# A slot planner that counts the piece it lets in, and VectorE pieces moved behind the slot's product

## The chip, the cores and the metric

The kernel runs on one NeuronCore of a Trainium2 chip, as one launch. The time is that of the device for the whole program, in microseconds (us). The engines are called by their short names: PE (TensorE), DVE (VectorE), ACT (ScalarE), POOL (GpSimd) and SP (SyncE, which here issues DMAs). Each engine has its own list of instructions and works it off in order; semaphores tie the lists together.

## The reference

Four images of 384 channels and 48 x 48 pixels in fp32 go through four layers. Each layer first normalises by groups of channels and adds its result to its input:

```python
x = x + mamba(_gn(x))        # L0: projections, a causal conv of 4 taps, a scan with 16 states, LayerNorm
x = x + fft_ffn(_gn(x))      # L1: 1x1 conv, 8x8 rfft2 * filter, irfft2, 3x3 depthwise, gelu gate, 1x1 conv
x = x + dwconv11(_gn(x))     # L2: depthwise 11x11 whose taps come from 4 moving points
x = x + moe(_gn(x))          # L3: 4 experts, two 1x1 convs each, top-2 routing over all pixels
```

The core of L0 runs over 2304 time steps for each of 768 channels and 16 states:

```python
dA = exp(dt * A); h = dA * h + dt * B * x; y = sum_over_states(h * C)
```

## The kernel before

**L0 in slots.** `scans` (from line 556) cuts each image into 5 chunks of 460 or 464 time steps, and each chunk into 96 slots. A slot is one state of one tile of 128 channels. There are 4 x 5 x 96 = 1920 slots. The order in which a slot's instructions stand is written out by hand in a loop (lines 1074 to 1113) under a manual schedule. In slot `u`: DVE runs the recurrence as one scan instruction (`scan`, L850); the product with C is made by DVE in the same slot (`product_now`, L870) in somewhat over half of the slots, and by POOL a slot later (`product`, L879) in the others, which are called slow; ACT copies the last column as carry (`keep`, L864) and makes the decay of a later slot by an exponential (`decay`, L826); POOL makes the driving term of slot `u + 3` (`drive`, L837); PE transposes and adds the product of slot `u - 3` or `u - 5` into a PSUM bank (`turned`, L770). The carry of a slot with a DVE product is copied after that product. The decay lies in PSUM; there are three such banks at most, and six buffers for g.

**Everything else is fed into the slots.** While image b + 1 is in L0, the later layers of image b fill the gaps: `later` (L1, L2 and the scores of L3) and `experts` (L3's experts 0 to 3). Their work is written as generators, called tasks. A task yields ahead of each step what the step is: `("act",)`, `("dve",)`, `("pool",)` or `("pe", weight, ring)`. The weight is an estimate of its time on PE in us. L0's own side work (projections, gates, output projection, LayerNorm) is written in the same way.

**Who lets a step in.** There are three lanes: `aux` (L0's own, not bound by the meter), `one` (`later`) and `two` (`experts`). `Lane.step` goes over its tasks and emits the next step of each that may go. One `Meter` (L62 to L69) keeps PE's backlog: every slot takes 2.3 off, adds 0.44 for the slot's own transposes, and each step let in adds its weight. A bound lane's PE step is let in while the backlog is not over 2.0; how large the step itself is isn't asked. A PE step also needs a free PSUM bank (`Ring`: three banks for pieces and one for accumulators; a bank is free again once its reader has been emitted). `Task.move` sets the slot from which the next step may go.

**Order within a slot** (lines 1080 to 1113): the lanes' ACT steps; collect; the scan; the transposes of earlier slots; the lanes' other steps, DVE's among them; the DVE product with its carry; decay; POOL's product; drive; DMA issues for B and C. So a lane's DVE step stands between the slot's scan and the slot's product.

**After the last slot**, lane `two` still holds expert blocks of image 2, and all later layers of image 3 remain. They are fed by the same lanes without scans (loop at lines 1816 to 1824), until the routing over all pixels (`route_all`) and the experts of image 3 (`all_experts`, L1709 and L1726) close the program. This stretch is called the tail below. A block of an expert is two products, `ph` and `pout`, of 9 matmuls each (L1609), every one of them two records in the profile.

The DVE steps that the change touches, each of which reads a PSUM tile that PE has written: `gate` (L907), the filter of L1 (L1225), the residual of L1 (L1311, L1313), that of L2 (L1437, L1439), an expert's bias (L1587) and an expert's sum (L1641 for experts 1 to 3, L1644 for expert 0).

Of the kernel before, what the change touches and what calls it, by code (L numbers as in the profile page):

```python
# [68 lines left out]
        self.value = max(0.0, self.value - self.each) + given  # L69


class Task:

# [3 lines left out]
        self.steps, self.next, self.ended, self.after = None, None, False, 0  # L79

    def move(self, slot=0):

        self.after = slot + 1 if self.next and self.next[0] == "act" else 0
        try:
            if self.steps is None:
                self.steps = self.make()
            self.next = (*next(self.steps), 0, None, None)[:4]
        except StopIteration:
            self.ended = True


class Lane:
# [4 lines left out]
        self.meter = meter  # L97
        self.bound = bound

    def step(self, act, slot, at=0):  # L100
        for task in self.active:
            if task.ended:
                continue
            kind, weight, ring, when = task.next
            if (kind == "act") != act or task.after > slot:
                continue
            if weight and self.bound and self.meter.value > self.meter.limit:
                continue
            if (ring and not ring[0].free(ring[1])) or (when and not when()):
                continue  # L110
            self.meter.value += weight
            task.move(slot)
        self.active = [t for t in self.active if not t.ended]
        while (
            self.queue and len(self.active) < self.width and self.queue[0].at <= max(at, slot)
            and all(t.ended for t in self.queue[0].needs)
        ):
            task = self.queue.pop(0)
            task.move()
            if not task.ended:  # L120
                self.active.append(task)

    def drain(self, slot, others=()):
        n = 0
        while self.queue or self.active:
            self.meter.value = 0.0
            for act in (True, False):
                for lane in (self, *others):
                    lane.step(act, slot + n, 1 << 30)
            n += 1  # L130
            assert n < 20000, "stuck"

# [7 lines left out]
def tile_layers(ctx: ExitStack, tc: tile.TileContext, a: dict, out: bass.AP):  # L140
# [272 lines left out]
    with ExitStack() as first:  # L413
# [142 lines left out]
        def scans(wk, mm, ring, meter, place, lanes, begin):  # L556
# [338 lines left out]
            def gate(i, m):  # L895
                (b, t), c = G[i], st[i]
                n = CHUNKS[t]
                w = n // TT
                yield ("pe", 0.45, (ring, 1))
                ps, r = ring.take(f"pyb{b}_{t}_{m}")  # L900
                for k in range(TT):
                    nc.tensor.transpose(
                        ps[:, bass.ts(k, w)], c["yt", m][:w, bass.ts(k, P)], ident[:w, :w]
                    )
                yield ("dve",)
                zm = c["zs"][:, m, :n]
                nc.vector.tensor_tensor(zm, ps[:, :n], zm, ALU.mult)  # L907
                ring.done(r)
# [134 lines left out]
            def ready(u):  # L1043

                i, p, m, s, _ = where(u)
                task, n = named.get(("steps", i, p)), 0
                while task and not task.ended:
                    for act in (True, False):
                        for lane in (aux, *lanes):
                            lane.step(act, u + n, 1 << 30 if lane is aux else 0)  # L1050
                    n += 1
                    assert n < 1000, "stuck"

# [9 lines left out]
            with tc.manual_schedule():  # L1063
                ordered[0] = True
                for k in range(3):
                    spread(k, 0)
                    spread(k, 1)
                for u in range(3):
                    drive(u)
                spread(3, 0)  # L1070
                for u in range(3):
                    decay(u)
                decays = 3
                for u in range(N + 6):
                    if u % LEN == 0 and u <= N:
                        plan(u // LEN, u)
                    if u < N and u % (LEN * NC) == 42 and u > 42:
                        begin(G[u // LEN][0])
                    place[0] = u
                    for lane in (aux, *lanes):  # L1080
                        lane.step(True, u)
                    for h, e in ((1, u - 4), (0, u - 5)):
                        if 0 < e < N and e % PAIR == PAIR - 1:
                            collect(e, h)
                    if u < N:
                        scan(u)


                    meter.slot(0.44)
                    early = u % PAIR >= 8  # L1090
                    if early:
                        add(u - 5, True)
                        add(u - 3, False)
                    for lane in (aux, *lanes):
                        lane.step(False, u)
                    if u < N:
                        product_now(u)
                    if decays < N and decays <= u + (3 if decays < LEN * NC else 2):
                        decay(decays)
                        decays += 1  # L1100
                    if 0 < u <= N:
                        product(u - 1)
                    if u + 3 < N:
                        ready(u + 3)
                        drive(u + 3)
                    if not early:
                        add(u - 5, True)
                        add(u - 3, False)
                    if u % 2:
                        spread((u + 7) // 2, 0)  # L1110
                        spread((u + 5) // 2, 1)

                at = u
                while aux.queue or aux.active:
                    at += 1
                    meter.slot(0.0)
                    for act in (True, False):
                        for lane in (aux, *lanes):
                            lane.step(act, at)
                lanes[0].drain(at, lanes[1:])  # L1120
                place[0] = at
                ordered[0] = False
# [4 lines left out]
        def later(b, ring, accr):  # L1127
# [71 lines left out]
            def patches(hb, wb):  # L1199
# [21 lines left out]
                us, uk = ufs.take(f"uf{u_}")  # L1221
                nc.tensor.matmul(ps[:, :C], lhsT=dft_f, rhs=ts_, start=True, stop=True)  # L1222
                tps.done(tk)
                yield ("dve",)
                nc.vector.tensor_tensor(us, ps[:, :C], filt_t, ALU.mult)  # L1225
                ring.done(r)
                yield ("pe", 0.65, (ring, 1))
# [24 lines left out]
            def finish_strip(hb):  # L1252
# [46 lines left out]
                for ct in range(CT):  # L1299
                    yield ("pe", 1.3, (ring, 1))  # L1300
                    ps, r = ring.take(f"pb{b}_{hb}_{ct}")
                    nc.tensor.matmul(  # L1302
                        ps[:, :LB], lhsT=w[:, 0, bass.ts(ct, P)], rhs=act[:, 0, :],
                        start=True, stop=False,
                    )
                    nc.tensor.matmul(  # L1306
                        ps[:, :LB], lhsT=w[64:P, 1, bass.ts(ct, P)], rhs=act[64:P, 1, :],
                        start=False, stop=True,
                    )
                    yield ("dve",)  # L1310
                    nc.vector.tensor_add(x[:, ct, :], ps[:, :LB], x[:, ct, :])  # L1311
                    ring.done(r)
                    nc.vector.bn_stats(stats2[b % 2][:, ct, hb, :], x[:, ct, :])  # L1313
# [92 lines left out]
            def windows(ct, k, r, first, last, final):  # L1406
# [24 lines left out]
                    for h in range(2):  # L1431
                        lines.done(d["row", ct, r, h][1])
                if last:
                    yield ("dve",)
                    n = BANDS[k] * W
                    x, xk = d["xb", ct, k]
                    nc.vector.tensor_add(x[:, :n], d["acc2"][0][:, :n], x[:, :n])  # L1437
                    accr.done(d["acc2"][1])
                    nc.vector.bn_stats(stats3[b % 2][:, ct, k, :], x[:, :n])  # L1439
                    yield ("pool",)  # L1440
                    nc.sync.dma_start(x3d[b][of_band(ct, k)], x[:, :n])
                    xbs.done(xk)
# [104 lines left out]
        def experts(b, ring, rings):  # L1547
# [15 lines left out]
            def begin(e):  # L1563
# [12 lines left out]
                for m in range(CT):  # L1576
                    for k in range(CT):
# [4 lines left out]
                            start=k == 0,  # L1582
                            stop=k == CT - 1,
                        )
                yield ("dve",)
                nb = d["nb", e] = small.tile([P, CT], F32, name=f"nb1_{b}_{e}", tag="nb1")
                nc.vector.tensor_tensor(nb, b1_all[:, e, :], ps[:, :CT], ALU.subtract)  # L1587
                ring.done(r)
# [13 lines left out]
            def block(s, e):  # L1602
# [30 lines left out]
                done(("h", s, e))  # L1633
                if s == NS - 1:
                    done(("w", e))
                yield ("dve",)
                key = ("y" if e else "x", s, e)
                x = d[key][0]
                if e:
# [134 lines left out]
            )  # L1774

        ring, accr = psum("mm", 3), psum("acc", 1)
        meter = Meter(2.3, 2.0)
        one, two = Lane(8, meter), Lane(4, meter)

        def begin(b):  # L1780
# [12 lines left out]
        with (  # L1793
# [6 lines left out]
            at = place[0]  # L1800
            while not all(ring.read):
                at += 1
                for act in (True, False):
                    two.step(act, at)
            two.queue = held

        rt = first.enter_context(tc.tile_pool(name="route", bufs=1))
        with (
# [7 lines left out]
            while one.queue or one.active or two.queue or two.active:  # L1816
                at += 1
                meter.slot(0.0)
                if not (one.queue or one.active):
                    meter.value = 0.0  # L1820
                for act in (True, False):
                    for lane in (one, two):
                        lane.step(act, at)
            coef, whole = route_all(rt, mm)
            all_experts(
                NB - 1, wk,
# [117 lines left out]
```

## Time and profile before

| | us |
|---|---|
| median of 3 runs | 5437.34 |
| lowest, highest | 5428.49, 5438.78 |
| profiled execution, its own time | 5425.31 |
| its span | 5423.4 |
| first scan starts | 86.9 |
| last scan ends | 4525.0 |
| PE busy over the span | 4666.9 (86%) |
| DVE busy | 4053.8 (75%) |
| POOL busy | 3365.2 (62%) |
| ACT busy | 2985.2 (55%) |

The profile is that of one execution. Its page gives busy time by engine, the span in 40 slices, and groups of instructions with their mean time; the trace behind it can be asked for any stretch. A wait is put down to the instruction that ended it. A stretch of 96 slots, one chunk of L0, is the natural unit here: its bounds are the starts of every 96th L850. Chunks are numbered 0 to 19. Chunks 0 to 4 are image 0 and have L0's own work alone; from chunk 5 on the lanes have work of the later layers as well.

### The profile page before, as it was taken

Reading aid. Unit: us, or ns where it says so; the run is one execution under the profiler, and the core shown is the slowest. Engines: PE = TensorE matmul, PEld = TensorE weight load, DVE = VectorE, ACT = ScalarE, POOL = GpSimd, SP = SyncE. Lnnn points to the kernel's source line nnn. Section 1 sums busy time; section 2 is a strip of 40 time slices with the busy share of each in tenths; the row PEclk is TensorE's granted clock in tenths of the full one; section 3 lists DMA queues with packets and bytes.
Section 4 is the critical chain, followed back from the end, with each engine's and each line's share of the span. In section 5 each row is a group of like instructions: output and inputs, shape, how many; then the busy total and the mean of one; then the engine's idle time right before and its main releaser. Section 6 shows DMA issues by size and latency. Waiting matters only on the chain. (4 is left out here: it accounts for less than half of the span.)

```text
span 5423.4 us, 81753 instructions
## 1 busy us (share of the span) xinstructions
PE 4666.9 (86%) x27796; PEld 3676.0 (68%) x27796; DVE 4053.8 (75%) x5581; ACT 2985.2 (55%) x6632; POOL 3365.2 (62%) x3020
## 2 busy tenths in 40 slices
PE   5677677687678988988789999988899999999899
PEld 4444454454347767665678887765678878889799
DVE  5999989889998788899887778899977674452200
ACT  3565565565558765655467655665566653334321
POOL 3878878876678788765667678775777673000000
PEclk8788788788789999999899999999999999999899
DMA  4445445454345555644566566554655554543200
GB/s 123 138 136 148 127 128 146 126 150 132 106 129 150 146 161 164 177 143 139 155 169 176 149 170 171 156 158 129 170 157 169 157 167 143 166 140 112 64 27 23
DMA packets 628391, 758.95 MB, mean 140 GB/s; under 512 B 58869, under 2 KB 622181, under 8 KB 627582
## 3 DMA queue, kind: packets, MB, share of 16 engines
q1 hardware_dynamic: 617668, 751.98, 48.2%
q8 instruction: 221, 3.62, 0.3%
q10 hardware_dynamic: 10298, 1.67, 0.2%
q14 instruction: 204, 1.67, 0.1%
HBM read 663.81 MB, written 89.65 MB: 139 GB/s over the span
## 5 line engine op out<-in xcount | busy, mean ns | idle before, releaser
L837 POOL TENSOR_TENSOR bu<-u,B 128x460 f32<-128x460 f32 (+1 forms) x1920 | 2227.5, 1170 | 778.2 <-DVE g L850 395.5
L826 ACT ACTIVATE da<-dt,a_neg 128x460 f32<-128x460 f32 (+1 forms) x1920 | 1242.8, 649 | 281.9 <-DVE g L870 185.4
L770 PE MATMUL y<-ident,g 128*115 128x128 f32 (+1 forms) x7680 | 1140.2, 297 | 274.1 <-DVE g L870 164.1
L770 PEld LDWEIGHTS y<-ident,g 128*115 128x115 f32 (+1 forms) x7680 | 1011.0, 187 | 502.3 <-DVE g L870 199.2
L879 POOL TENSOR_TENSOR g<-g,C 128x460 f32<-128x460 f32 (+1 forms) x885 | 1030.5, 1164 | 276.8 <-ACT carry L864 270.4
L850 DVE TENSOR_TENSOR_SCAN da<-da,carry,bu 128x460 f32<-128x460 f32 (+1 forms) x828 | 971.3, 1173 | 133.3 <-ACT da L826 94.7
L850 DVE TENSOR_TENSOR_SCAN g<-da,carry,bu 128x460 f32<-128x460 f32 (+1 forms) x708 | 819.7, 1167 | 83.5 <-ACT da L826 35.3
L870 DVE TENSOR_TENSOR g<-da,C 128x460 f32<-128x460 f32 (+1 forms) x1035 | 653.9, 632 | 91.7 <-PE y L770 31.5
L864 ACT COPY carry<-da 128x1 f32<-128x1 f32 x828 | 130.5, 158 | 824.3 <-DVE g L870 821.2
L1609 PE MATMUL pout<-hr,we 128*128 128x144 f32 x3456 | 483.6, 296 | 41.7 <-ACT hr L1625 31.7
L1609 PEld LDWEIGHTS pout<-hr,we 128*128 128x128 f32 x3456 | 455.4, 196 | 64.9 <-ACT hr L1625 42.6
L1609 PE MATMUL ph<-xe,we 128*128 128x144 f32 x3456 | 470.1, 291 | 13.4 <-DMA xe<-x3d 7.5
L1609 PEld LDWEIGHTS ph<-xe,we 128*128 128x128 f32 x3456 | 446.8, 194 | 30.6 <-issue 7.6
L1416 PE MATMUL pc<-band,row 128*128 128x162 f32 (+14 forms) x3456 | 458.8, 287 | 6.3 <-ACT row L1403 6.0
L1416 PEld LDWEIGHTS pc<-band,row 128*128 128x128 f32 x3456 | 446.2, 196 | 11.9 <-ACT row L1403 7.5
L1274 DVE SCALAR_TENSOR_TENSOR dw<-pad,w_dw,dw 128x384 f32<-128x384 f32 x576 | 347.6, 614 | 17.6 <-ACT pad L1249 6.7
L642 PE MATMUL pin<-xch,w_inx 128*128 128x463 f32 (+2 forms) x720 | 327.9, 595 | 34.7 <-DMA xch<-in_x 15.2
L921 PE MATMUL po<-w_out,zs 128*115 128x384 f32 (+1 forms) x960 | 341.5, 499 | 6.9 <-DVE dt L750 6.4
L1625 ACT ACTIVATE hr<-ph,nb 128x144 f32<-128x144 f32 x576 | 176.4, 377 | 305.2 <-PE ph L1609 303.6
L674 PE MATMUL pinz<-xch,w_inz 128*128 128x460 f32 (+1 forms) x720 | 316.8, 578 | 0.0
L1383 ACT ACTIVATE rep<-x,br,wr 128x192 f32<-128x192 f32 x576 | 274.3, 541 | 4.2 <-issue 4.2
L661 DVE SCALAR_TENSOR_TENSOR xc<-pin,conv_w,xc 128x460 f32<-128x460 f32 (+1 forms) x360 | 249.2, 692 | 30.9 <-ACT xc L655 19.2
(202 smaller groups left out, 5797.6 us busy)
## 6 DMA issues: line engine op xcount, KB each, us to landing
B<-bcd SPq DMA_DIRECT2D x768, 230.0 KB, 3.5
C<-bcd SPq DMA_DIRECT2D x768, 230.0 KB, 3.7
B<-bcd SPq DMA_DIRECT2D x192, 232.0 KB, 3.7
C<-bcd SPq DMA_DIRECT2D x192, 232.0 KB, 4.2
xe<-x3d SPq DMA_DIRECT2D x192, 216.0 KB, 2.8
ye<-y3d SPq DMA_DIRECT2D x144, 216.0 KB, 2.8
y3d<-ye SPq DMA_DIRECT2D x96, 216.0 KB, 2.2
xs<-x1d SPq DMA_DIRECT2D x24, 576.0 KB, 4.6
```

The costliest lines, as they stand in the source:

```text
L642: nc.tensor.matmul(ps[:, lo : halo + n], lhsT=w_inx[:, k, bass.ts(j, P)], rhs=c["x"][:, k, lo : halo + n], start=k == 0, stop=k == CT - 1,)
L674: nc.tensor.matmul(ps[:, :n], lhsT=w_inz[:, k, bass.ts(j, P)], rhs=c["x"][:, k, DCONV - 1 : DCONV - 1 + n], start=k == 0, stop=k == CT - 1,)
L770: nc.tensor.matmul(c["y", m][:w, bass.ts(k, P)], lhsT=src[:, bass.ts(k, w)], rhs=ident, is_transpose=True, start=c["terms", m] == 1 and k ...
L826: nc.scalar.activation(da[:, :n], c["dt", p][:, m % 2, :n], AF.Exp, scale=a_neg[:, m, s : s + 1])
L837: nc.gpsimd.tensor_mul(bu[:, :n], c["u", p][:, m % 2, :n], live["B", u // 2][:, :n])
L850: nc.vector.tensor_tensor_scan(here[:, :n], da[:, :n], bu[:, :n], last if t else nil[:, 0:1], ALU.mult, ALU.add,)
L870: nc.vector.tensor_mul(live["g", u][:, :n], live["h", u][:, :n], live["C", u // 2][:, :n])
L879: nc.gpsimd.tensor_mul(g[:, :n], g[:, :n], live["C", u // 2][:, :n])
L921: nc.tensor.matmul(ps[:w, :C], lhsT=c["zs"][:, m, bass.ts(k, w)], rhs=w_out0[:, m, :], start=m == 0, stop=m == MT - 1,)
L1274: nc.vector.scalar_tensor_tensor(v, src, w_dw[:, ct, k : k + 1], v, ALU.mult, ALU.add)
L1416: nc.tensor.matmul(d["acc2"][0][:, : BANDS[k] * W].rearrange("p (h w) -> p h w", w=W)[:, lo - edges[k] : hi - edges[k], xlo:xhi], lhsT=d[" ...
L1609: nc.tensor.matmul(ps[:, bass.ts(m, EB)], lhsT=w[:, k, bass.ts(m, P)], rhs=of[:, k, :], start=k == 0, stop=k == CT - 1,)
```

## The change

Three things are changed.

1. `Lane.step` compares the backlog with the piece's weight added, `value + weight > limit`, and the limit goes from 2.0 to 3.7.
2. A third phase is added to each slot. DVE steps that read what PE has made for them yield `("late",)`, and the lanes' late steps are emitted after `product_now`. DVE's other steps stay ahead of the product.
3. `Task.move` holds every kind of step, and not ACT's alone, to one a slot, so that a PE step and its late reader do not fall into one slot.

```diff
+PHASE = {"act": 0, "late": 2}
...
     def move(self, slot=0):
-
-        self.after = slot + 1 if self.next and self.next[0] == "act" else 0
+        self.after = slot + 1 if self.next else 0
...
-    def step(self, act, slot, at=0):
+    def step(self, phase, slot, at=0):
         for task in self.active:
             if task.ended:
                 continue
             kind, weight, ring, when = task.next
-            if (kind == "act") != act or task.after > slot:
+            if PHASE.get(kind, 1) != phase or task.after > slot:
                 continue
-            if weight and self.bound and self.meter.value > self.meter.limit:
+            if weight and self.bound and self.meter.value + weight > self.meter.limit:
                 continue
...
                     for lane in (aux, *lanes):
-                        lane.step(True, u)
+                        lane.step(0, u)
...
                     for lane in (aux, *lanes):
-                        lane.step(False, u)
+                        lane.step(1, u)
                     if u < N:
                         product_now(u)
+                    for lane in (aux, *lanes):
+                        lane.step(2, u)
...
-        meter = Meter(2.3, 2.0)
+        meter = Meter(2.3, 3.7)
```

In `gate`, `patches`, `finish_strip`, `windows`, `experts.begin` and `block`, the step ahead of the lines named above changes in the same way:

```diff
-                yield ("dve",)
+                yield ("late",)
```

All other loops over phases (`drain`, `ready`, the loops of the tail) go over three phases in place of two.

More of the change, by code (lines that the diff above doesn't have):

```diff
@@ L126, in drain @@
             self.meter.value = 0.0
-            for act in (True, False):
+            for phase in range(3):
                 for lane in (self, *others):
-                    lane.step(act, slot + n, 1 << 30)
+                    lane.step(phase, slot + n, 1 << 30)
             n += 1
@@ L1047, in ready @@
                 while task and not task.ended:
-                    for act in (True, False):
+                    for phase in range(3):
                         for lane in (aux, *lanes):
-                            lane.step(act, u + n, 1 << 30 if lane is aux else 0)
+                            lane.step(phase, u + n, 1 << 30 if lane is aux else 0)
                     n += 1
@@ L1116, in scans @@
                     meter.slot(0.0)
-                    for act in (True, False):
+                    for phase in range(3):
                         for lane in (aux, *lanes):
-                            lane.step(act, at)
+                            lane.step(phase, at)
                 lanes[0].drain(at, lanes[1:])
@@ L1223, in patches @@
                 tps.done(tk)
-                yield ("dve",)
+                yield ("late",)
                 nc.vector.tensor_tensor(us, ps[:, :C], filt_t, ALU.mult)
@@ L1309, in finish_strip @@
                     )
-                    yield ("dve",)
+                    yield ("late",)
                     nc.vector.tensor_add(x[:, ct, :], ps[:, :LB], x[:, ct, :])
@@ L1433, in windows @@
                 if last:
-                    yield ("dve",)
+                    yield ("late",)
                     n = BANDS[k] * W
@@ L1584, in begin @@
                         )
-                yield ("dve",)
+                yield ("late",)
                 nb = d["nb", e] = small.tile([P, CT], F32, name=f"nb1_{b}_{e}", tag="nb1")
@@ L1635, in block @@
                     done(("w", e))
-                yield ("dve",)
+                yield ("late",)
                 key = ("y" if e else "x", s, e)
@@ L1802, in tile_layers @@
                 at += 1
-                for act in (True, False):
-                    two.step(act, at)
+                for phase in range(3):
+                    two.step(phase, at)
             two.queue = held
@@ L1820, in tile_layers @@
                     meter.value = 0.0
-                for act in (True, False):
+                for phase in range(3):
                     for lane in (one, two):
-                        lane.step(act, at)
+                        lane.step(phase, at)
             coef, whole = route_all(rt, mm)
```

## Prediction

> **What bounds the kernel now.** I read the page's busy times and slices first, then the busy times by stretch of 96 slots, then the waits of DVE and ACT, then one place in order of time. From the page:
>
> ```profile
> PE 4666.9 (86%) x27796; PEld 3676.0 (68%) x27796; DVE 4053.8 (75%) x5581; ACT 2985.2 (55%) x6632; POOL 3365.2 (62%) x3020
> PE   5677677687678988988789999988899999999899
> DVE  5999989889998788899887778899977674452200
> PEclk8788788788789999999899999999999999999899
> ```
>
> DVE leads early, PE later, PE alone at the end. The second view has stretch, length and PE, PEld, DVE, ACT, POOL busy; the stretches are chunks 11, 12, 13, 14, 19 and the tail.
>
> ```profile
> 2358.10:2625.20 267.10, 227.47 (x1211) 163.13 (x1210) 247.27 (x356) 147.53 (x337) 173.20 (x157) 0.94 0.50 148
> 2625.20:2876.40 251.20, 216.66 (x1342) 174.49 (x1343) 206.29 (x281) 149.81 (x350) 172.47 (x153) 0.93 0.57 159
> 2876.40:3117.10 240.70, 231.89 (x1604) 200.15 (x1603) 179.30 (x229) 169.94 (x402) 172.31 (x154) 0.97 0.56 161
> 3117.10:3338.00 220.90, 209.60 (x1328) 165.17 (x1328) 175.16 (x228) 130.29 (x235) 171.49 (x152) 0.95 0.62 174
> 4309.40:4525.00 215.60, 206.16 (x1426) 176.12 (x1425) 164.27 (x209) 118.09 (x227) 167.77 (x149) 0.95 0.63 179
> 4525.00:5423.40 898.40, 857.43 (x6343) 791.92 (x6341) 233.15 (x515) 287.19 (x736) 4.59 (x15) 0.97 0.31 90
> ```
>
> Chunk 11 (L1's taps) is DVE's, 13, 14 and 19 are PE's, 12 is neither's: 251 us against 217 and 206. The tail is PE's. Over chunks 5 to 19 the length exceeds the busier of PE and DVE by 11 to 35 us a chunk, about 275 us in all: that is what a better order can reach. The waits there, 1016.5 to 4525 us (total, times, longest):
>
> ```profile
> DVE da L850 <- ACT da L826: 103.0, 78, 8.1
> DVE ye L1641 <- PE pout L1609: 82.8, 58, 3.9
> DVE xe L1644 <- PE pout L1609: 17.1, 18, 3.3
> DVE xb L1437 <- PE pc L1416: 15.7, 16, 1.8
> ACT carry L864 <- DVE g L870: 605.2, 340, 6.2
> ```
>
> One place shows the chain (start, length, [idle before]):
>
> ```profile
> 2963.38 4.10 PE L1609 MATMUL pout<-hr,we 128*128 128x144 f32 x18
> ...
> 2967.52 0.61 DVE L1641 TENSOR_TENSOR ye<-pout,ye 128x432 f32<-128x432 f32 x1 [2.55 <-PE pout L1609]
> 2968.05 0.62 DVE L870 TENSOR_TENSOR g<-da,C 128x460 f32<-128x460 f32 x1
> ...
> 2968.59 1.17 DVE L850 TENSOR_TENSOR_SCAN da<-da,carry,bu 128x460 f32<-128x460 f32 x1
> ...
> 2968.70 0.16 ACT L864 COPY carry<-da 128x1 f32<-128x1 f32 x1 [4.84 <-DVE g L870]
> ```
>
> DVE waits for `pout`, though the slot's product behind it is ready; ACT's carry waits for that product, and the decay behind the carry. PE was at half clock here (0.50 from 2961 to 2965), after 2.4 us of idleness.
>
> [...] the granted clock over chunks 5 to 19 shows 64 half-speed stretches, 524 us long. [...]
>
> **Part 1, the backlog with the piece counted.** Rows give for one matmul of the program (two records) 0.276 us for L1609 ((483.6 + 470.1) / 3456), 0.265 for L1416 (458.8 / 1728), 0.309 for L1395 (133.3 / 432), 0.33 for L1578 (35.4 / 108). I counted both programs' PE orders by chunk. Nothing moves up to chunk 6. L2's windows come earlier and the experts later: chunk 13 gains 72 L1416 and 21 L1395 and loses 108 L1609 (19.1 + 6.5 - 29.8 = -4). So: chunk 7 +10, 8 +3, 9 +9, 10 -15, 11 -7, 12 +5, 13 -4, 14 -11, 15 -1, 16 -3, 17 +4, 18 -1, 19 -30. The sum is -42 us, and the tail gets it: 8 more blocks (62 become 70) and 9 more L1578, one expert's bias.
>
> In the tail the matmuls run at full clock, 25 us for 207 records in the all-experts part, 0.121 us each: 8 x 36 x 0.121 = 35, with the bias 38 us, all on the path, since PE is 95% busy there. In the scans I count what a chunk gains in full where PE leads clearly (8, 10, 13, 14, 15, 18: -29), at half where both are close (9, 12, 17: +9), at two thirds in 19 (-20; DVE's 164 us stop it), and not at all where DVE leads (7, 11, 16). That gives -40. Bounds: -15, if only chunks 13, 14 and half of 19 give, to -50. Taken: -40 + 38 = -2.
>
> The part also evens PE's load. By the meter's own ledger, slots with over 3.5 us of work fall from 62 to 14, those over 4 from 15 to none; slots with no more than about 1.2 us, where PE runs dry, from 450 to 421 (of chunk 6 and on). The spread of a slot's load falls by 16 to 26% in chunks 12, 13, 17 and 18; I use 17%. If the excess over the busier engine falls with it: 35 us of chunk 12 give 6, 23 of chunk 17 give 4, 9 each of 13 and 18 give 3, together -13; I take -12. Half-speed stretches cost half their length; in the chunks that PE leads (8 to 10, 12 to 15, 17 to 19) that is 108 us, and 6% fewer dry slots give -7. Both could be nothing, or reach -50 if whole chains of stalls go. The reverse, +10, comes if less fill leaves PE idle and at half clock more often.
>
> **Part 2, late pieces.** No work is added. I went through the scans: 472 DVE instructions of this kind, 131 of which waited, 167 us in all. 212 stand ahead of a product in their slot. The product (0.63 us) can now be done in such a wait; the smaller of wait and product, summed, is 34.5 us, the upper bound. In chunks that PE leads DVE's wait is only the echo of PE's pace. The rest (image 0 with 3 us, and 5, 6, 7, 9, 11, 12, 16, 17) holds 14 us. I take -8, since ACT's decay may be late next. Against it: what is queued behind a late piece now is the next scan, which waited for it before too; and its PSUM bank comes free a product later, up to 0.63 us. A PE piece that wants that bank then stands a slot later, which is in the counts above. ACT's carry comes up to a late piece (0.6 to 1.3 us) earlier, which helps the decay: in the -8. POOL's and SP's lists change order at most beside the moved pieces; POOL's has idle time (172 of some 240 us busy), so nothing is charged.
>
> **Part 3, one step a slot.** A PE step was already visited once a slot and its reader a slot later. Only where `ready` runs ahead would it delay steps; its effect is in the orders. Nothing is charged.
>
> **Sum.** 5425.3 - 2 - 12 - 7 - 8 = 5396 for the profiled execution; the median of the runs stood 12 us above that, so 5408.
>
> **Rivals.**
> *The tail pays in full and the scans give little back (slower).* For: chunk 19 loses 30 us of PE work but DVE's 164 us and the ACT chain may hold it at its pace[...]. Against: PE was 95% busy there. With -15 from the scans, nothing from evening and -5 from part 2: 5437 + 38 - 20 = 5455. It decides if the last scan ends later than 4525 - 38 = 4487.
> *The chains of stalls break (much faster).* For: 605 us of ACT's waits and 246 us of DVE's waits for ACT or transposes hang on them. Against: in PE-led chunks PE's own idleness is only some 10 us. Half of the 108 us of half clock, and 25 us of part 2: 5437 - 2 - 54 - 25 = 5356.
> *It cancels out.* The order does change, as the counts show, but stalls move from the late piece to the scan, which waits for it anyhow, and work moves from one PE-led stage into another: 5437, within 0.2%.
>
> **How the numbers follow.** Forecast (5380 to 5426) 0.46; much faster 0.14; cancelled 0.19; slower 0.21. The range, 5368 to 5458, leaves out the outer part of the two outer cases. A measurement of this kernel can tell about 0.2% (11 us) from no change. Faster 0.60, same 0.19, slower 0.21.
>
> **What would show it.** The last scan should end near 4525 - 40 - 27 = 4458 and the tail be near 936 us. Chunk 19 shortens most, 10 and 14 next; 7, 11 and 16 hardly. DVE's wait for `pout` at L1641 and L1644 falls below 80 us in the scans, and ACT's carry waits less than 605. I am wrong if the last scan ends after 4487, if the tail grows by much else than 38 us, or if the half-speed stretches increase.

## The result and the profile after

The changed kernel takes 5458.02 us (median of 6 runs, 5449.51 to 5463.46) against 5431.21 us before (6 runs, 5423.22 to 5438.78). The ratio is 1.0049, with a 95% interval of 1.0033 to 1.0065: slower by half a per cent. The profiled execution took 5452.64 us, with a span of 5450.8 us. Lines are numbered 3 to 5 higher in the changed kernel, so that L1609 is now L1614, L1641 is L1646 and L870 is L873.

The page of the changed kernel, the lines that answer to those of before:

```profile
PE 4658.3 (85%) x27796; PEld 3665.8 (67%) x27796; DVE 4062.2 (75%) x5581; ACT 2989.4 (55%) x6632; POOL 3362.8 (62%) x3020
PE   5677677677678989988799899988899998999899
DVE  5999989889997788899977788899978772641200
PEclk8788788798789989999899999999999999999899
```

Every engine has as many instructions as before. PE is busy 9 us less, DVE and ACT 8 and 4 us more, and the span is 27 us longer: what PE lost is idle time. The view by stretch says where (stretch, length, then PE, PEld, DVE, ACT and POOL busy, and last PE's granted clock as a share of full speed, the DMA engines' busy share and GB/s). The first line is chunks 5 to 19 together, then come chunks 7, 11, 12, 13, 14, 17 and 19, and the tail.

```profile
1019.40:4512.10 3492.70, 3052.14 (x18053) 2355.76 (x18054) 2947.22 (x3959) 2133.78 (x4717) 2583.00 (x2312) 0.93 0.53 153
1485.60:1718.90 233.30, 184.00 (x985) 135.14 (x986) 199.54 (x269) 148.51 (x333) 169.14 (x151) 0.86 0.44 129
...
2374.30:2640.10 265.80, 223.59 (x1158) 163.30 (x1158) 246.92 (x355) 147.73 (x333) 172.98 (x157) 0.92 0.50 148
2640.10:2880.30 240.20, 215.28 (x1333) 173.07 (x1334) 204.71 (x279) 156.63 (x363) 171.52 (x152) 0.93 0.54 156
2880.30:3124.90 244.60, 229.77 (x1596) 194.41 (x1596) 181.16 (x231) 173.92 (x408) 173.27 (x155) 0.97 0.54 156
3124.90:3341.80 216.90, 205.07 (x1310) 160.65 (x1310) 174.68 (x227) 118.33 (x213) 172.61 (x154) 0.98 0.64 178
3825.80:4071.80 246.00, 218.14 (x1335) 175.01 (x1334) 203.01 (x275) 155.28 (x359) 171.66 (x152) 0.93 0.52 151
...
4308.50:4512.10 203.60, 188.49 (x1249) 156.33 (x1249) 161.14 (x204) 104.73 (x194) 168.07 (x149) 0.95 0.66 188
4512.10:5450.80 938.70, 894.26 (x6635) 830.09 (x6633) 238.93 (x524) 295.94 (x760) 4.25 (x14) 0.97 0.33 93
```

The same view of the kernel before, for chunks 5 to 19, 7 and 17, which were not shown:

```profile
1016.50:4525.00 3508.50, 3096.55 (x18345) 2402.92 (x18346) 2947.38 (x3968) 2137.96 (x4743) 2585.13 (x2312) 0.93 0.54 154
1482.30:1706.10 223.80, 172.03 (x881) 126.53 (x882) 198.81 (x268) 142.18 (x318) 169.25 (x151) 0.84 0.45 131
3826.10:4060.10 234.00, 211.00 (x1314) 168.40 (x1313) 202.96 (x280) 150.59 (x350) 171.34 (x152) 0.95 0.59 164
```

The tail grew by 40.3 us (938.7 against 898.4). In chunks 5 to 19 PE is busy 44.4 us less, but the length fell by 15.8 us only: length less PE's busy time, so PE's idleness, went from 411.9 to 440.6 us. That is 28.6 us, and it is about the whole loss (the spans differ by 27.4), since what PE's busy time lost and what the tail gained nearly cancel. By chunk, 12, 18 and 19 gave back 11 to 13 us each; 7 and 17 took 10 and 12 more, and chunk 9 took 11. L2 begins in 7, 12 and 17 alike, so that alone does not decide.

DVE's waits in the same stretch (total, times, longest):

```profile
DVE da L853 <- ACT da L829: 101.2, 69, 8.1
DVE g L873 <- PE y L773: 60.4, 42, 9.3
...
DVE g L873 <- DMA C<-bcd: 40.0, 23, 6.6
...
DVE xb L1442 <- PE pc L1421: 21.9, 20, 3.5
...
DVE ye L1646 <- PE pout L1614: 21.6, 26, 2.2
```

The wait at the experts' sum fell as forecast, from 82.8 to 21.6 us. But the product waits more than before: 60.4 us for PE's transposes, which free the buffer it writes, and 40.0 us for the C rows. The same lines before, and one of ACT's carry:

```profile
DVE g L870 <- PE y L770: 31.1, 33, 2.9
...
DVE g L870 <- DMA C<-bcd: 9.9, 9, 2.4
...
ACT carry L864 <- DVE g L850: 100.6, 134, 2.8
```

Only part of this stands where a piece was moved. In the changed kernel's list of DVE, 15 of the 42 waits for the transposes, 14.3 us, have a late piece behind the product in their slot; the other 27 have none. ACT's carry in the changed kernel:

```profile
ACT carry L867 <- DVE g L873: 549.4, 335, 5.1
ACT carry L867 <- DVE g L853: 147.2, 165, 2.5
```

The first line was 605.2 and the second 100.6: of the 56 us that the product no longer costs ACT, the scan costs it 47. Last, PE's own waits in the changed kernel, four of the lines that rose:

```profile
PE pout L1614 <- ACT hr L1630: 38.7, 24, 3.9
...
PE pin L645 <- DVE xc L664: 16.6, 6, 4.5
PE ph L1614 <- DMA xe<-x3d: 15.9, 9, 3.7
PE pc L1421 <- ACT row L1408: 15.8, 9, 8.1
```

and the same four before:

```profile
PE pout L1609 <- ACT hr L1625: 21.4, 17, 3.5
...
PE pc L1416 <- ACT row L1403: 6.0, 5, 3.2
...
PE ph L1609 <- DMA xe<-x3d: 4.7, 5, 1.9
...
PE pin L642 <- DVE xc L661: 2.4, 2, 1.6
```

In three of them PE comes to a lane's piece before the input is there. `pin`, a projection of L0, waits for the DVE instruction that reads an earlier `pin` out of its PSUM bank. Other lines fell: the transposes' wait for DVE's product (`y` <- `g`) from 43.9 to 38.9 us, that of `pt` for ACT from 26.8 to 19.8.

### The profile page after: what moved, and what is told of

Read it like the earlier page. It is cut to its first block, busy times and chain, and to the rows that moved or that the text cites. A ratio compares the mean times of both kernels' runs of the same rounds, so it can differ in the third digit from the quotient of the medians.

```text
span 5450.8 us, 81823 instructions
## 1 busy us (share of the span) xinstructions
PE 4658.3 (85%) x27796; PEld 3665.8 (67%) x27796; DVE 4062.2 (75%) x5581; ACT 2989.4 (55%) x6632; POOL 3362.8 (62%) x3020
## 5 line engine op out<-in xcount | busy, mean ns | idle before, releaser
L773 PE MATMUL y<-ident,g 128*115 128x128 f32 (+1 forms) x7680 | 1126.6, 294 | 250.3 <-DVE g L873 158.6
L773 PEld LDWEIGHTS y<-ident,g 128*115 128x115 f32 (+1 forms) x7680 | 997.9, 185 | 461.5 <-DVE g L873 194.4
L873 DVE TENSOR_TENSOR g<-da,C 128x460 f32<-128x460 f32 (+1 forms) x1035 | 656.6, 634 | 160.8 <-PE y L773 60.7
L1614 PE MATMUL pout<-hr,we 128*128 128x144 f32 x3456 | 481.6, 295 | 51.6 <-ACT hr L1630 47.5
L1614 PE MATMUL ph<-xe,we 128*128 128x144 f32 x3456 | 490.9, 299 | 29.2 <-DMA xe<-x3d 19.2
L1614 PEld LDWEIGHTS pout<-hr,we 128*128 128x128 f32 x3456 | 452.3, 195 | 78.3 <-ACT hr L1630 61.1
L1614 PEld LDWEIGHTS ph<-xe,we 128*128 128x128 f32 x3456 | 465.9, 201 | 44.8 <-issue 7.9
L1421 PE MATMUL pc<-band,row 128*128 128x162 f32 (+14 forms) x3456 | 454.4, 285 | 19.6 <-ACT row L1408 15.8
```

The source lines that it names most:

```text
L773: nc.tensor.matmul(c["y", m][:w, bass.ts(k, P)], lhsT=src[:, bass.ts(k, w)], rhs=ident, is_transpose=True, start=c["terms", m] == 1 and k ...
L873: nc.vector.tensor_mul(live["g", u][:, :n], live["h", u][:, :n], live["C", u // 2][:, :n])
L1421: nc.tensor.matmul(d["acc2"][0][:, : BANDS[k] * W].rearrange("p (h w) -> p h w", w=W)[:, lo - edges[k] : hi - edges[k], xlo:xhi], lhsT=d[" ...
L1614: nc.tensor.matmul(ps[:, bass.ts(m, EB)], lhsT=w[:, k, bass.ts(m, P)], rhs=of[:, k, :], start=k == 0, stop=k == CT - 1,)
```

## The experiments

Every run was timed in five rounds beside the kernel before on the same chip, whose medians lay between 5424.67 and 5429.66 (5431.21 beside the change itself). "Blocks" are the expert blocks that stay for the tail, counted in the built programs. The last three columns are of one profiled execution each: PE busy and idle in chunks 5 to 19 (idle is length less busy), and the tail.

| run | blocks | median us | ratio (95%) | PE busy | PE idle | tail |
|---|---|---|---|---|---|---|
| before | 62 | 5431.21 | | 3097 | 412 | 898 |
| the change | 70 | 5458.02 | 1.0049 (1.0033 to 1.0065) | 3052 | 441 | 939 |
| meter_only | 66 | 5438.67 | 1.0018 (1.0008 to 1.0029) | 3087 | 421 | 912 |
| late_only | 64 | 5459.26 | 1.0060 (1.0045 to 1.0075) | 3089 | 433 | 913 |
| bank_late | 64 | 5455.82 | 1.0052 (1.0038 to 1.0066) | 3090 | 428 | 912 |
| after_bank | 70 | 5445.51 | 1.0030 (1.0018 to 1.0043) | 3052 | 430 | 938 |
| late_uf | 62 | 5427.78 | 1.0000 (0.9992 to 1.0008) | 3094 | 410 | 902 |
| late_ye | 62 | 5423.89 | 0.9998 (0.9987 to 1.0009) | 3099 | 402 | 902 |
| after_l45 | 54 | 5448.49 | 1.0031 (1.0020 to 1.0042) | 3146 | 419 | 877 |
| before_e26 | 58 | 5470.53 | 1.0081 (1.0064 to 1.0098) | 3118 | 442 | 895 |
| before_l16 | 71 | 5438.08 | 1.0022 (1.0015 to 1.0029) | 3049 | 426 | 935 |
| before_l19 | 64 | 5468.43 | 1.0080 (1.0064 to 1.0095) | 3109 | 432 | 907 |
| before_l24 | 60 | 5458.44 | 1.0065 (1.0050 to 1.0080) | 3109 | 438 | 890 |
| before_e21 | 78 | 5491.24 | 1.0126 (1.0107 to 1.0144) | 3033 | 466 | 973 |
| before_b40 | 64 | 5445.76 | 1.0037 (1.0024 to 1.0050) | 3097 | 417 | 910 |
| before_b44 | 64 | 5450.31 | 1.0042 (1.0027 to 1.0057) | 3089 | 423 | 912 |
| after_b40 | 70 | 5458.59 | 1.0060 (1.0043 to 1.0077) | 3064 | 434 | 940 |
| after_b44 | 70 | 5456.31 | 1.0054 (1.0035 to 1.0072) | 3055 | 440 | 939 |
| after_exslack_l45 | 65 | 5447.24 | 1.0038 (1.0025 to 1.0052) | 3092 | 434 | 898 |
| after_slack_l45 | 66 | 5425.95 | 0.9996 (0.9985 to 1.0007) | 3087 | 439 | 905 |

### One part alone, and a price for a block

My first theory was the prediction's slower rival: blocks go to the tail at full price and the scans give little back, so that the time follows the number of blocks.

`meter_only`, on the kernel before:

```diff
-            if weight and self.bound and self.meter.value > self.meter.limit:
+            if weight and self.bound and self.meter.value + weight > self.meter.limit:
...
-        meter = Meter(2.3, 2.0)
+        meter = Meter(2.3, 3.7)
```

> Only the meter is changed (weight counted in, limit 3.7); DVE's late steps and the hold of one step a slot are as before. Its tail holds 66 expert blocks (62 before, 70 with the whole change). Theory A, a block moved into the tail costs 5 us there and gives back about 2 us in the scans: 4 blocks more, +13 us, about 5444. Theory B, the order with late pieces is what costs and the meter alone is harmless or helps by evening the load: 5415 to 5431. Tail length by A: 898 + 20 = 918 us.

It took 1.0018 of the time before, some 10 us more. `late_only` is the reverse of it on the changed kernel:

```diff
-            if weight and self.bound and self.meter.value + weight > self.meter.limit:
+            if weight and self.bound and self.meter.value > self.meter.limit:
...
-        meter = Meter(2.3, 3.7)
+        meter = Meter(2.3, 2.0)
```

> Only the late phase and the hold of one step a slot are in; the meter is as before (backlog not over 2.0). Its tail holds 64 expert blocks. Theory A: 2 blocks more, about +7 us less what the late order saves (0 to 8), 5430 to 5438. Theory B, late pieces cost in the scans (a PSUM bank held a product longer, a piece a slot later): +20 us or more, over 5450, with the scans longer than before at equal work.

It took 1.0060 of the time before, all that the whole change takes, with two blocks more than before and not eight. The parts do not add up either. `after_l45`, on the changed kernel:

```diff
-        meter = Meter(2.3, 3.7)
+        meter = Meter(2.3, 4.5)
```

> The whole change, with the limit at 4.5 in place of 3.7. Its tail holds 54 expert blocks, 16 fewer than with 3.7 and 8 fewer than before. Theory A: 8 blocks fewer than before, -27 us, about 5404, with a tail near 860 us and scans about 15 us longer than before. Theory B: the scans' order costs as it did, the time stays within 10 us of the changed kernel's 5458. Theory C, bursts on PE are what costs: the higher limit brings them back, the scans grow by 40 us or more and the time is 5435 or above.

`before_e26`, on the kernel before:

```diff
-        meter = Meter(2.3, 2.0)
+        meter = Meter(2.6, 2.0)
```

> The kernel before with one number changed: the meter takes 2.6 us off a slot in place of 2.3, so that more PE work is let into the scans. Its tail holds 58 expert blocks, 4 fewer than before. It asks for the price of a moved block with nothing else changed. Theory A: -13 us, about 5418. If PE's time in the scans is worth as much as in the tail (as the prediction had it, -40 against +38): 5431, no change.

Both have fewer blocks in the tail than before, and both are slower, by 19 and 41 us. The first theory falls: the time doesn't follow the number of blocks. Theory C, that bursts on PE cost, had asked for longer scans and a time over 5435 in `after_l45`. Both came, but they don't single it out: the scans are 73 us longer than the changed kernel's with 94 us more of PE's busy time, while PE's idleness is 22 us less.

### The order on DVE, and the plan

A late piece does two things: it stands behind the product on DVE, and its PSUM bank counts as free a phase later, so that PE's pieces are placed differently, that is, in other slots. Where all pieces stand is called the plan below. `bank_late` keeps the second and drops the first: on the kernel before, a bank counts as free at the end of the slot.

```diff
+    def later(self, k):
+        HELD.append((self, k))
...
-                ring.done(r)
+                ring.later(r)
...
                     if u < N:
                         product_now(u)
+                    release()
```

In the built programs PE, ACT, POOL and SP have the same lists in `bank_late` as in `late_only`, instruction for instruction.

> The plan of the late phase without its order on DVE: the six kinds of DVE pieces stand ahead of the slot's product as before, but a PSUM bank counts as free only at the slot's end. PE, ACT, POOL and SP have exactly the lists of the run with the late phase alone (5459), with 64 expert blocks in the tail; DVE's list alone differs. Theory D, the order on DVE costs, since PE waits for pieces that now stand behind the product (L1225 above all, 31 us more there): 5430 to 5440. Theory E, the plan costs (banks held longer, pieces a slot later): about 5455 to 5460, the same as with the late order. The prediction's part 2 would have the late order gain 8 here, so this at 5467.

The view by stretch, chunks 5 to 19 and tail, of `late_only`:

```profile
1014.90:4536.00 3521.10, 3088.51 (x18321) 2396.55 (x18322) 2956.94 (x3967) 2136.70 (x4738) 2585.03 (x2312) 0.93 0.53 154
4536.00:5449.10 913.10, 866.18 (x6366) 798.42 (x6366) 233.22 (x517) 289.58 (x739) 4.29 (x14) 0.97 0.31 90
```

and of `bank_late`:

```profile
1017.80:4535.40 3517.60, 3090.04 (x18320) 2397.60 (x18320) 2952.01 (x3967) 2135.71 (x4738) 2584.70 (x2312) 0.93 0.53 154
4535.40:5447.80 912.40, 864.88 (x6367) 798.07 (x6366) 233.29 (x516) 289.15 (x739) 4.28 (x14) 0.97 0.31 90
```

They agree within 4 us in both stretches. The order on DVE is worth nothing here; the loss comes with the placing, which the two kernels share. `after_bank` is the same edit together with the change of the meter, so that DVE's list alone differs from the changed kernel:

> The whole change with DVE's six kinds of pieces back ahead of the product, and banks free at the slot's end: PE, ACT, POOL and SP as in the changed kernel, 70 expert blocks in the tail, DVE's list alone differs. Theory D: 20 to 30 below the changed kernel, 5430 to 5440. Theory E: 5455 to 5465. Prediction's part 2: 5466.

It stands 18.7 us above the kernel before that ran beside it, where the changed kernel stands 26.8 above its own: some 8 us less, with intervals of the ratios that overlap. Under this plan the late order may cost a little. It doesn't gain in either plan.

`late_uf` and `late_ye` make one kind of piece late on the kernel before: the filter of L1 (its list of PE is that of before), and the experts' pieces (PE's list differs from that of before in 1,171 of 20,782 places).

```diff
-                yield ("dve",)
+                yield ("late",)
```

> The kernel before with one of the six kinds late, the filter of L1 (L1225, 54 pieces in the scans, none of which waited before). PE, ACT, POOL and SP as before, 47 places of DVE's list change. Theory D: PE's next step waits for it, +10 to +20. Theory E or the prediction: no change, within 5 of 5429.

> The kernel before with the experts' pieces alone late (L1641, L1644, L1587, which had 115 of the 167 us of waits). The tail holds 62 blocks as before. If the product fills these waits as the prediction had it: -10, 5420. If the product must wait for the same late PE (its own transposes free the buffer it writes) the wait only moves: within 5 of 5429.

Neither moves the time. DVE's waits in `late_ye`:

```profile
DVE ye L1646 <- PE pout L1614: 62.0, 45, 3.8
DVE g L873 <- PE y L773: 44.7, 38, 4.0
DVE xe L1649 <- PE pout L1614: 12.8, 15, 2.6
```

The experts' pieces wait 25 us less than before (74.8 against 99.9), and the product waits 14 us more for PE. Six of the product's waits, 12.9 us, stand just ahead of an experts' piece. So half of the gain has only moved, and the rest buys nothing. The third part of the change needs no run: with it alone, no step being late, all five lists are those of the kernel before.

### Other placings with the old rules

If the placing makes the loss, is it a bad one, or is that of before a good one? Four kernels change one number of the kernel before: the limit (2.0) to 1.6, 1.9 or 2.4, or the amount taken off per slot (2.3) to 2.1.

```diff
-        meter = Meter(2.3, 2.0)
+        meter = Meter(2.3, 1.6)
```

> The kernel before with its limit at 1.6 in place of 2.0; nothing is counted in and no piece is late. 71 expert blocks stay for the tail, one more than with the whole change. Theory F, work taken out of the scans comes back in full in the tail (5 us a block) while the scans shorten by about a third of it, since PE then waits for its own inputs: +25 to +30, 5453, with PE idle over 430 us in chunks 5 to 19 (410 before). The prediction's step, the scans give back what they lose: 5427, no change.

> The kernel before with its limit at 1.9: a nudge. 64 blocks in the tail. Theory F: +7, 5434. Theory G, the plan of before is a lucky one and any plan beside it is 10 to 30 slower whatever its block count (PE idle 420 to 440): 5437 to 5457.

> The kernel before with its limit at 2.4: 60 blocks in the tail, 2 fewer. Theory F with a price as in the tail: -7, 5420. Theory G: 5437 to 5457. A knee at the load of before (the run with 2.6 us a slot and 58 blocks took 41 more): 5440 or more, with PE busy 10 us more and the scans 20 us longer or more.

> The kernel before with the meter taking 2.1 us off a slot: 78 blocks in the tail, 16 more. It asks for the price of removal on a long lever. Theory F: tail +80, scans -27 to -35, 5475. The prediction's step (-40 against +38 for 8 blocks): 5427. Theory G adds 10 to 30 whatever the count: 5437 to 5457.

All are slower. The smallest nudge, 1.9, takes 44 us; the larger one to 1.6, which leaves 71 blocks for the tail where the change leaves 70, takes 13. Theory F falls: it had asked for 7 us at 1.9 and for 25 to 30 at 1.6. A knee at the load of before, the other reading of 2.4 and of `before_e26`, doesn't explain the four either: 1.9 lets less into the scans than before, and is slower too. The view by stretch of `before_l19`:

```profile
1017.00:4558.30 3541.30, 3109.44 (x18321) 2405.42 (x18322) 2952.25 (x3967) 2134.95 (x4739) 2585.55 (x2312) 0.92 0.53 153
4558.30:5465.50 907.20, 862.59 (x6366) 797.66 (x6366) 233.70 (x516) 289.00 (x739) 4.29 (x14) 0.97 0.31 90
```

It has 24 records fewer on PE in the scans than before (18321 against 18345), and takes 33 us longer over them: PE is idle 20 us longer, and busy 13 us longer although its records are fewer.

The last test leaves all rules and numbers of the meter alone, and lets the later layers enter two slots earlier or later:

```diff
-                    if u < N and u % (LEN * NC) == 42 and u > 42:
+                    if u < N and u % (LEN * NC) == 40 and u > 40:
```

> The kernel before, with the later layers of an image entering the lanes in slot 40 of the next image in place of 42. Every rule is as before; 64 blocks in the tail (62). Theory G, the placing that before has is a lucky draw: 5437 to 5465, PE idle in chunks 5 to 19 at 420 to 440. If the rules of before make its quality, +0 to +10 for two blocks: 5425 to 5435 and PE idle near 410.

> As the run with slot 40, with slot 44: 64 blocks in the tail. Theory G: 5437 to 5465. The rules of before make its quality: 5425 to 5435.

> The whole change with the later layers entering in slot 40 in place of 42; 70 blocks in the tail as with 42. Theory G, the change has only drawn another placing: anywhere from 5430 to 5470, different from the changed kernel's 5455 by 10 or more, and no worse on average than the two shifted kernels of before. If the change's rules cost: 5450 to 5460 again.

> As the run with slot 40 and the whole change, with slot 44; 70 blocks in the tail. Theory G: 5430 to 5470, not worse on average than the shifted kernels of before. The change's rules cost: 5450 to 5460.

With the old rules the shift costs 1.0037 and 1.0042; with the new ones the three entries stand at 1.0060, 1.0049 and 1.0054. Theory G had asked for a scatter among the new ones, 10 us or more from the changed kernel, and this did not come: both shifted kernels lie where the rival, that the rules themselves cost, had put them (5450 to 5460). `before_b40`:

```profile
1015.40:4529.40 3514.00, 3096.89 (x18323) 2405.69 (x18323) 2951.84 (x3967) 2136.44 (x4741) 2584.84 (x2312) 0.93 0.53 154
4529.40:5439.10 909.70, 864.83 (x6365) 798.89 (x6364) 233.93 (x517) 287.68 (x736) 4.29 (x14) 0.97 0.31 89
```

So a shift by two slots, either way and with no new rule, loses 20 to 25 us, nearly the 27 of the change. What the rules add on average is less clear. Against the two shifted kernels it is 1.0054 less 1.0040, about 8 us. With slot 42, which is the kernel before itself, counted among the old rules too, it is 1.0054 less 1.0026, about 15 us. Three entries a side do not separate either from nothing, nor do they show that the rules cost nothing.

### More room between an input and its reader

In most of these runs PE stands idle longer before the matmuls of the lanes' own pieces (L1, L2 and the experts: 136 us before, 184 in the changed kernel, 165 to 204 in all other kernels of the table but `late_uf` and `late_ye`). The last theory was that PE comes to them too early. Two kernels give more room, with the limit raised to 4.5 so that the lanes keep up: `after_exslack_l45` puts one empty slot between an expert's relu and the product that reads it, and `after_slack_l45` holds every PE step that follows an ACT step one slot more.

```diff
+def SLACK(was, now):
+    return was == "act" and now == "pe"
...
+        was = self.next and self.next[0]
...
+            if SLACK(was, self.next[0]):
+                self.after = slot + 2
```

> The whole change, with one idle slot put between an expert's relu on ACT and the product that reads it, and the limit at 4.5 so that 65 blocks stay for the tail. Theory J, PE reaches the lanes' pieces before their inputs are there because the evened backlog is shorter, the experts' product above all (75 us of PE's idleness stand before the experts' matmuls in the changed kernel, 43 before): that falls below 45, PE's idle time in chunks 5 to 19 below 415, and the time to 5430 or less. If it only moves: idle time at 420 to 440 and 5440 or more.

> The whole change, with every PE step that follows an ACT step of its task held one slot more, and the limit at 4.5 (66 blocks in the tail). Theory J: PE's idleness before pieces of L1, L2 and the experts (184 us in the changed kernel, 136 before) falls below 130, and the time to 5430 or less. If it only moves: 5440 or more.

The first is at 1.0038: PE's idleness before the experts' products `ph` and `pout` fell from 68 us in the changed kernel to 49, but its whole idleness is 434 us, against 441. It has mostly moved. The second is at 0.9996: it makes good the whole loss, as fast as before and no faster. But not for the reason given: in its profile (an execution of 5439.01 us, 13 above its median) PE's idleness before those pieces is 204 us and not under 130, and PE's whole idleness 439 us. The theory falls, although the time came out. Nor does this profile show where the time was won. The edit also holds L0's own steps, and chunk 5 starts at 1005.7 us here against 1016.5 before: 11 us are gained where the lanes have no work yet.

## Why the prediction was wrong, point by point

The forecast was 5408 us, 29 below the 5437 of the three runs then known; measured are 5458, 27 above the 5431 of six runs.

- **What bounds the kernel.** PE at the end and DVE and PE by turns before it: this held. That chunk 7 is DVE's, so that PE work put there is free, was wrong. It got 12 us more of PE's busy time and became 9.6 us longer. A chunk's mean hid its second half: there PE (89.7 us) and DVE (91.5) were about even before, in 107.4 us, and there the change brought PE to 100.3 and the length to 116.4.
- **The tail, +38.** Measured +40.3. Right.
- **The scans give back 40.** As PE's busy time they did, 44.4 us less, but partly by luck. PE was busy at half speed (a granted clock of 0.50) for 390.6 us of chunks 5 to 19 before and for 358.4 after. In the kernel before, the 18 records of the `pout` at 3896.18 us, at 0.50 throughout, took 4.69 us, and those of the one at 3887.26 us, at full clock throughout, 2.37. Counting half of the half-speed time as lost, an estimate from these four figures, 16 of the 44 us are less half speed and only 28 are work that left. Chunk 19 lost 18 us of busy time where 30 were forecast. Busy time out of the scans and length of the tail nearly cancel (-4.1; -2 was forecast). As length they gave 15.8, since idleness came in its place.
- **Evening the load, -12, half clock, -7, and late pieces, -8.** This is the step that failed: evening and late pieces were to cut the waits that are left in the scans, and in the sum nothing was charged for new ones (+10 was named as the reverse, and not taken). In place of their -20 there stand 28.6 us of added idleness of PE. With the meter alone (`meter_only`) PE's idleness is 421 us, no less than the 402 to 412 of the three kernels with the old plan or nearly it: evening shows no gain. The half-speed stretches became more (71 against 64) but shorter in sum (469 us against 524), so the gain at half clock did come, within the busy time above. For late pieces I wrote of one place that the product behind the wait is ready. It wasn't. PE's transposes there:

```profile
2967.32 1.04 PE L770 MATMUL y<-ident,g 128*115 128x128 f32 x8
```

The first four of these transposes free the product's buffer, and they ended at 2967.92 us, 0.44 us after `pout`. That is not the rule, though. Of the 38 waits at the experts' sums ahead of a product, 52.3 us in chunks 5 to 19 of the kernel before, PE had already done what the product needs when 31 of them began (43.5 us). So waits could be filled, and `late_ye` filled some; the time didn't gain by it. With the plan held equal, dropping the late order moves the time by -1 us in one pair (`bank_late` +29.0 above its before, `late_only` +30.1) and by -8 in the other (`after_bank` +18.7, the change +26.8): no gain for the late order in either, and no sure loss.
- **One step a slot, nothing.** Right, and exactly so.
- **PSUM banks.** I saw that a bank comes free a product later and priced it at nothing, since the counts held it. The counts hold where a piece goes, not what it meets there, and so this zero had no ground. `bank_late` shows 29 us for this alone, and the shifted entries show that 20 to 25 us are lost by moving the plan in another way, with no bank held longer.
- **The rivals.** The slower one had the number (5455), its deciding point (the last scan ended at 4512.1, after 4487) and its 15 us from the scans. Its mechanism as a rule for blocks fell: 71 blocks cost 13 us in one plan, 58 cost 41 in another; that its number fits is partly luck. The cancelling one had stalls move elsewhere, as half of them do in `late_ye`, but not the added idleness.
- **Small slips in the reading.** By the views of before, the length exceeds the busier of PE and DVE by 9 to 35 us a chunk, not 11 to 35 (chunks 13, 18 and 19 are at 9), and the list of changes by chunk sums to -41, not -42. Nothing hangs on either.

What stays open is what makes the placing of before good. The runs hold seventeen other kernels with fifteen other lists of PE, the changed kernel among them (`late_uf` and `late_ye`, which leave PE's list alone or nearly so, are not counted; they equal the kernel before). Of the seventeen `after_slack_l45` equals it too, the other sixteen are 10 to 67 us slower, and none is faster. That the loss of the late pieces comes with the placing is shown by `bank_late`, and that placing alone can cost as much by the shifted entries; why it costs PE idle time is only located (PE waits longer for inputs of the lanes' pieces, on ACT and DMA), not explained. Two readings stay open: that the new rules place pieces worse wherever the layers enter, or that before is an unusually good plan, perhaps because its numbers had been chosen by its time. No run here tells them apart.

## What to carry to other kernels

When an edit to a scheduler moves thousands of instructions, price it by its redraw too: shift the whole plan by a slot or two with the old rules and see how the time spreads. Here that spread, 20 us and more, was nearly as large as the effect to be forecast, and all on the slow side. Split the busy time of the leading engine, too, into work and slower clock, and keep its idle time apart. And ahead of claiming that a ready instruction can fill a wait, look at what that instruction itself waits for: at the place shown, both waited for PE.

## What was not expected of the hardware

In chunks 5 to 19 of the kernel before, 64 stretches at a granted clock of 0.50 begin: 24 of them last 3.41 us, 23 last 6.83 us and 7 last 10.24 us. In the changed kernel it is 42, 15 and 8 of 71. Ahead of the routing, PE stood idle for 12.9 us in the changed kernel (from 5132.2 us), and 1.4 us into this gap a half-speed stretch of 30.7 us began. At the place shown in the prediction, a gap of 2.4 us ended at 2960.12 us, and a half-speed stretch of 6.8 us had begun 0.2 us ahead of its end. Of PE's gaps in chunks 5 to 19 of the kernel before that began at full clock, 17 of 31 between 1.5 and 2 us had a half-speed stretch begin in them or within 3.5 us after them, 10 of 12 between 2.4 and 3 us, and 15 of 16 of 3.5 us and more. In these counts the length of a gap alone doesn't decide.
